# A scan kernel's broadcast load, taken from two stored copies, with its partitions ordered images by states

## The chip, the core and the metric

The kernel runs on one core of a Trainium2 chip. The metric is the device time of one execution in microseconds (us), as the median of several executions of the same build. The engines are named as in the profile: PE (matmul) and PEld (its weight load), DVE (vector), ACT (scalar activation), POOL (the general engine, here used for element-wise products) and SP, which issues nearly all DMAs. Sixteen DMA engines move the data of the core.

## What is computed

Four layers follow one another on 64 images of 11 x 11 = 121 tokens with 128 channels. Each layer is a mixer (a normalisation, then a state-space model) and a feed-forward part. Only the mixer is touched by the change. Its core, cut from the reference:

```python
xc = silu(conv1d(x @ in_proj_w.T) + conv_b)       # 121 rows d, 256 places l
delta = softplus(einsum('bkrl,kdr->bkdl', dts, dt_proj_w) + dt_proj_b)
dA  = exp(delta[..., None] * A)                   # 16 states n
dBu = delta[..., None] * Bs * xs[..., None]
h   = associative_scan(h[l] = dA[l] * h[l-1] + dBu[l], axis=l)
y   = einsum('bkdln,bknl->bkdl', h, Cs) + Ds * xs
y   = y[:, 0] + flip(y[:, 1])                     # two directions k
out = layer_norm(y) * gelu(z) @ out_proj_w.T
```

For each image b, direction k and row d there are 16 states n, each with a recurrence over 256 places.

## The kernel before

**Tiling.** A mixer treats the 64 images in 8 chunks c of 8 images. A chunk and a direction make one m (16 in a mixer). The 128 partitions hold 16 states times 8 images. In one step, `scan` (L701) runs the recurrence for two rows d on DVE: 128 partitions x 512 elements. An m has 61 steps, so a chunk has 122 and a mixer 976.

**What a step needs.** `rows` (L680) brings delta to the 128 partitions: a matmul of `pick` (a 0/1 matrix made in `made`, L148) with the tile `R`, into one of five PSUM tiles `da`. `exps` (L694) turns it into dA on ACT with the scale `A`, which is loaded with a broadcast over images (L135). The other factor starts as u = delta * x, in the layout rows d on partitions (`steps`, L293, product on POOL at L333). It is stored to DRAM in `uD` by `store` (L360). `load_u` (L658) reads four rows d of it for 8 images, 4 KB for each image, and writes them to all 128 partitions of a tile `ub`: one DMA of 512 KB, of which 31 belong to an m. `times_b` (L671) multiplies the tile in place by the tile `Bt` on POOL, and two steps of `scan` consume it. There are six `ub` tiles (`UB`); a load is issued 10 steps ahead of its first scan (`lu`) and the product 5 steps ahead (`tb`).

**After the scan.** `by_c` (L716) contracts the states with matmuls whose weights are `Cz`. These are made by `own_c` (L648) on POOL from the tile `Cp` and the mask `own` (L171), which says which partition belongs to which image. `keep_y` (L737) gathers the results in `yst`, `store_y` (L755) writes them to DRAM, and `tail` (L453) reads them back as `y` for the norm, the gate and the output product. `load_bc` (L640) loads `Bt` and `Cp`, `load_r` (L628) the tiles `R`, of which there are two.

**Order.** The order is written by hand. `run` (L779) files every piece of work under a step number; the numbers come from the table `AT` (L87). In each step the code issues in this order: work filed as `pre`, the matmuls and the first exp of three steps ahead, the loads and products of `ub`, the scan, the planned work, the second exp. Each engine executes its own instructions in that order. The work of the next chunk (normalisation, convolution, softplus, stores of `dD` and `uD`) and the tail of the previous one are spread over the 122 steps of a chunk, so a steady chunk repeats the same pattern. SP issues all these DMAs from one queue, in order, and waits ahead of each for its tiles: a `ub` load waits until DVE has scanned the tile six loads before.

Of the kernel before, what the change touches and what calls it, by code (L numbers as in the profile page):

```python
# [8 lines left out]
F32 = mybir.dt.float32  # L9
BF16 = mybir.dt.bfloat16  # L10
AF = mybir.ActivationFunctionType
ALU = mybir.AluOpType
AX = mybir.AxisListType
# [3 lines left out]
D = 121  # L17
C = 128
L = 256
NS = 16  # L20
# [20 lines left out]
def bcast(ap, n):  # L41

    return ap.unsqueeze(2).to_broadcast([ap.shape[0], ap.shape[1], n])
# [27 lines left out]
def act_tables(nc, which):  # L71
# [8 lines left out]
CB = 8  # L80
# [4 lines left out]
RING = 5  # L85
UB = 6
AT = {  # L87
    "x": -12.5, "st": -3, "mv": 3, "sc2": 6, "sc3": 8, "nm": 10, "tn": 13.5, "td": 15.5, "tn2": 17.5,
    "td2": 19.5, "cv": 20, "cve": 49, "silu": 52, "p0": 53, "pa0": 3.75, "s0": 66, "b0": 66, "ba0": 7.875,
    "p1": 100, "pa1": 2.25, "s1": 109, "b1": 111, "ba1": 7.5, "u": 4, "d0": 1, "r": 3, "d1": 5, "l": 6.5,  # L90
    "d2": 7, "dst": 12.5, "bc": 54, "bca": 3, "sk": 99, "ska": 2.5, "y0": 15.5, "y1": 35, "y2": 57.5, "y3": 82,
    "k0": 27, "k1": 44.5, "k2": 66.5, "k3": 89, "ka": 2, "ks": 2.5, "km": 4.5, "k2s": 6.5, "k3s": 9, "kn": 11,
    "kg": 13, "xa": 28.5, "xb": 66, "g0": 38, "z0": 77, "g1": 81.5, "z1": 109, "ga": 5, "za": 3.5, "gt": 117.5,
    "gta": 2, "ge": 126.5, "cz": 8, "cza": 3.75, "lbc": -18, "lu": 10, "tb": 5, "ys": 8, "ysa": 1, "ysh": 8,
    "r0": -10, "r1": 2, "r2": 23, "r3": 37,
}


class Conv:
# [9 lines left out]
    def weights(self, setup, fixed, ps):  # L109
        cx, nc, a = self.cx, self.nc, self.cx.a  # L110
        p = f"L{self.l}_conv_"

        def load(pool, name, shape, src):
            t = pool.tile(shape, F32, name=name)
            nc.sync.dma_start(t, src)
            return t

        in_x = load(setup, "in_x", [128, 2, C], a[p + "in_x"].rearrange("(q p) c -> p q c", p=128))
        conv_wT = load(
            setup, "conv_wT", [128, 3, 2, L], a[p + "conv_wT"].rearrange("j (q p) o -> p j q o", p=128)  # L120
        )
        x_dt = load(setup, "x_dt", [8, 2, D], a[p + "x_dt"])
        dt_wT = load(setup, "dt_wT", [8, 2, D], a[p + "dt_wT"])
        self.Ds = fixed.tile([128, 2], F32, name="Ds")
        nc.vector.memset(self.Ds, 0.0)
        nc.sync.dma_start(self.Ds[:D], a[p + "Ds"])
        self.in_zT = load(fixed, "in_zT", [C, L], a[p + "in_zT"])
        self.conv_b = load(fixed, "conv_b", [1, L], a[p + "conv_b"])
        self.x_bc = load(fixed, "x_bc", [D, 4 * NS], a[p + "x_bc"])
        self.norm = load(fixed, "norm", [D, 2], a[p + "norm"])  # L130
        self.out_wT = load(fixed, "out_wT", [128, 2, C], a[p + "out_wT"].rearrange("(q p) c -> p q c", p=128))

        self.A = fixed.tile([128, 2, D], F32, name="A")
        for k in range(2):
            nc.sync.dma_start(self.A[:, k, :], a[p + "A_logs"][k].unsqueeze(1).to_broadcast([NS, CB, D]))  # L135
        return lambda: self.made(setup, fixed, ps, in_x, conv_wT, x_dt, dt_wT)

    def made(self, setup, fixed, ps, in_x, conv_wT, x_dt, dt_wT):
        cx, nc, a = self.cx, self.nc, self.cx.a
        p = f"L{self.l}_conv_"  # L140
        af = self.A.rearrange("p k d -> p (k d)")
        nc.scalar.activation(af, af, AF.Exp)
        nc.vector.tensor_scalar_mul(af, af, -1.0)


        pick = setup.tile([5 * 24, 5, CB], F32, name="pick")
        nc.vector.reduce_sum(pick, cx.ident[:120, :120].rearrange("p (a s b) -> p a b s", s=3, b=CB), axis=AX.X)
        self.pick = fixed.tile([5 * 24, 5, NS, CB], BF16, name="pick16")  # L148
        for i in range(5):
            nc.vector.tensor_copy(self.pick[:, i], pick[:, i, :].unsqueeze(1).to_broadcast([120, NS, CB]))  # L150

        self.w_conv = fixed.tile([C, 3, L], F32, name="w_conv")
        for j in range(3):
            pw = ps.tile([C, L], F32, name="pw", tag="mm")
            for q in range(2):
                nc.tensor.matmul(pw, in_x[:, q, :], conv_wT[:, j, q, :], start=(q == 0), stop=(q == 1))
            nc.scalar.copy(self.w_conv[:, j, :], pw)


        self.w_dt = fixed.tile([D + 1, 2, 128], F32, name="w_dt")  # L160
        nc.vector.memset(self.w_dt, 0.0)
        nc.sync.dma_start(self.w_dt[D : D + 1, :, :D], a[p + "dt_b"].unsqueeze(0))
        for k in range(2):
            pw = ps.tile([D, D], F32, name="pdt", tag="mm")
            nc.tensor.matmul(pw, x_dt[:, k, :], dt_wT[:, k, :], start=True, stop=True)
            nc.scalar.copy(self.w_dt[:D, k, :D], pw)
        self.ones = fixed.tile([1, 128], F32, name="ones")
        nc.vector.memset(self.ones, 1.0)

        self.own = fixed.tile([128, CB], F32, name="own")  # L170
        nc.vector.reduce_sum(self.own, cx.ident.rearrange("p (n b) -> p b n", b=CB), axis=AX.X)  # L171

    def buffers(self, fixed, work, ps_f, dram):
        cx, nc, NC = self.cx, self.nc, self.NC
        self.work = work

        self.H = [fixed.tile([128, 2 * L, 16], F32, name="H"), cx.HX.rearrange("p (a w) -> p a w", w=16)]
        self.spare = [x.rearrange("p a w -> p (a w)") for x in self.H]
        self.da = [ps_f.tile([128, 2, L], F32, name=f"da{i}") for i in range(RING)]
        self.yb = ps_f.tile([128, 8, 2, 2, 16], F32, name="yb")  # L180
        nc.vector.memset(self.yb, 0.0)
        self.Cz = [fixed.tile([128, 64, CB], F32, name=f"Cz{i}") for i in range(4)]
        self.t = fixed.tile([128, CB, L], F32, name="t")
        nc.gpsimd.memset(self.t, 1.0)  # L184
        self.xnT = [fixed.tile([C, CB, D + 2], F32, name=f"xnT{i}") for i in range(2)]
        for x in self.xnT:
            nc.gpsimd.memset(x[:, :, 0 : D + 2 : D + 1], 0.0)
        self.skip = [fixed.tile([D, CB, L], F32, name=f"skip{i}") for i in range(2)]
        self.yst = fixed.tile([128, 64, D], F32, name="yst")
        self.uD = dram.tile([NC, 2, CB, 128, L], F32, name="uD")  # L190
        self.dD = dram.tile([NC, 2, 128, 3, CB, L], BF16, name="dD")
        self.bcD = dram.tile([NC, 4 * NS, CB, L], F32, name="bcD")
        self.yD = dram.tile([NC, L, CB * D], F32, name="yD")
# [99 lines left out]
    def steps(self, c, k, at=None):  # L293


        nc, work, out = self.nc, self.work, []
# [7 lines left out]
        for b in range(0, CB, 2):  # L304
            s = {}
# [53 lines left out]

            def store(b=b, s=s):  # L360
                nc.sync.dma_start(self.dD[c, k, :, :, b : b + 2, :].rearrange("d s b l -> d s (b l)"), s["d"])
                nc.sync.dma_start(
                    self.uD[c, k, b : b + 2].rearrange("b d l -> d b l"), s["u"].rearrange("p (b l) -> p b l", l=L)
                )

            i = b // 2
            fs = (u, first, rest, second, less, third, store)
# [272 lines left out]
    def load_bc(self, m):  # L640
        c, k = m // 2, m % 2
        for name, at in (("Bt", 0), ("Cp", NS)):
            x = self.work.tile([128, L], F32, name=name, bufs=2)
            r0 = 2 * NS * k + at
            self.nc.sync.dma_start(x, self.bcD[c, r0 : r0 + NS].rearrange("r b l -> (r b) l"))
            self.bc[m, name] = x

    def own_c(self, m, u):  # L648
# [9 lines left out]
    def load_u(self, T):  # L658
        m, i = divmod(T, TILES)
        n = min(4, D - 4 * i)  # L660
        x = self.work.tile([128, 4, L], F32, name="ub", bufs=UB)
        self.ub[T] = x
        self.nc.sync.dma_start(
            x[:, :n, :].rearrange("p d l -> p (d l)"),
            self.uD[m // 2, m % 2, :, 4 * i : 4 * i + n, :]
            .rearrange("b d l -> b (d l)")
            .unsqueeze(0)
            .to_broadcast([NS, CB, n * L]),
        )

    def times_b(self, T):  # L671
# [8 lines left out]
    def rows(self, g):  # L680

        m, p = divmod(g, PAIRS)
        for j in range(self.channels(p)):
            d = 2 * p + j
            n = 24 if d == D - 1 else 120
            self.nc.tensor.matmul(  # L686
                self.da[g % RING][:, j, 1:],
                self.pick[:n, d % 5].rearrange("p n b -> p (n b)"),
                self.R[m, d // 35][:n, d % 35 // 5, 1:],
                start=True,  # L690
                stop=True,
            )
# [802 lines left out]
```

## Time and profile before

| | |
|---|---|
| median of 3 runs | 7740.06 us (7738.5 to 7741.94) |
| profiled execution, own time | 7752.68 us |
| its span, first to last instruction | 7750.9 us |
| mean granted TensorE clock | 0.85 |
| PE, DVE, ACT, POOL busy, share of the span | 78%, 73%, 70%, 68% |
| DMA queue of SP, share of 16 engines | 76.3%, 1521.09 MB in 903223 packets |
| HBM read, written | 1265.98 MB, 256.97 MB |

The shares are averages over four mixers and four feed-forward parts. The mixers take about three quarters of the span. In a steady chunk (steps 122 to 975 of a mixer without the last chunk) the engines are far busier than the averages, so stretches of such a chunk have to be read by themselves. The chunk that is used below as the example runs from 2460.69 to 2643.87 us, in the second mixer.

### The profile page before, as it was taken

What the parts mean: (1) busy time and instruction counts of PE and PEld (TensorE: products, weight loads), DVE (VectorE), ACT (ScalarE), POOL (GpSimd) and SP (SyncE); (2) the same over time, 40 slices, a digit from 0 to 9 for tenths busy, and PEclk for the clock granted to TensorE, in tenths of its full rate; (3) what the DMA queues carried; (4) which work ended last, traced back from release to release, by engine and by line L of the source; (5) the groups of instructions that cost most, each with busy time, mean ns of one, the idle gap of its engine ahead of it and who ended that gap; (6) DMA issues with size and microseconds to landing.
All of it is one profiled execution on the core that took longest, in us unless ns stands there. A gap on an engine that the chain in (4) does not pass through costs nothing. (4 is left out here: it accounts for less than half of the span.)

```text
span 7750.9 us, 208787 instructions
## 1 busy us (share of the span) xinstructions
PE 6041.0 (78%) x84334; PEld 3448.5 (44%) x84334; DVE 5659.8 (73%) x7849; ACT 5449.4 (70%) x12343; POOL 5293.3 (68%) x2659
## 2 busy tenths in 40 slices
PE   6788778776788877766788888767678887758999
PEld 3444444465344444444344444434344444434445
DVE  5888888844788888962788888871788888872201
ACT  7888888733888888853788888862788888852200
POOL 6798999812888888931888888940888898960000
PEclk8888898777898989875889989875788888879999
DMA  7899999856899999942899999951899999971111
GB/s 181 227 247 243 245 246 243 215 167 170 221 241 249 246 240 244 247 110 75 220 241 244 246 248 243 243 140 37 217 236 243 243 245 241 245 184 46 35 39 36
DMA packets 905471, 1536.54 MB, mean 198 GB/s; under 512 B 136840, under 2 KB 617442, under 8 KB 904503
## 3 DMA queue, kind: packets, MB, share of 16 engines
q1 hardware_dynamic: 903223, 1521.09, 76.3%
q8 instruction: 662, 10.85, 0.6%
q14 instruction: 306, 2.51, 0.1%
q10 hardware_dynamic: 1280, 2.10, 0.1%
HBM read 1265.98 MB, written 256.97 MB: 196 GB/s over the span
## 5 line engine op out<-in xcount | busy, mean ns | idle before, releaser
L675 POOL TENSOR_TENSOR ub<-ub,Bt 128x1024 f32<-128x1024 f32 (+1 forms) x1984 | 4557.2, 2323 | 589.7 <-DMA ub<-uD 447.1
L699 ACT ACTIVATE da<-da,A 128x255 f32<-128x255 f32 x7744 | 3291.7, 451 | 696.1 <-PE da L686 612.0
L707 DVE TENSOR_TENSOR_SCAN H<-da,ub 128x512 f32<-128x512 f32 x2048 | 2391.8, 1208 | 354.4 <-POOL ub L675 183.9
L707 DVE TENSOR_TENSOR_SCAN HX<-da,ub 128x512 f32<-128x512 f32 (+1 forms) x1856 | 2130.4, 1190 | 318.5 <-POOL ub L675 160.1
L686 PE MATMUL da<-R,pick 120*128 120x255 bf16 x7744 | 1658.9, 305 | 546.0 <-DVE H L707 277.3
L686 PEld LDWEIGHTS <-pick 120*128 120x128 bf16 x7744 | 662.9, 103 | 1494.6 <-issue 1054.9
L728 PE MATMUL yb<-H,Cz 128*16 128x64 f32 x32768 | 782.2, 236 | 187.7 <-ACT yst L745 107.7
L728 PE MATMUL yb<-HX,Cz 128*16 128x64 f32 x32768 | 813.4, 237 | 122.6 <-DVE HX L707 62.7
L728 PEld LDWEIGHTS yb<-HX,Cz 128*16 128x16 f32 x32768 | 531.3, 105 | 641.9 <-issue 338.1
L728 PEld LDWEIGHTS yb<-H,Cz 128*16 128x16 f32 x32768 | 540.9, 103 | 584.0 <-issue 313.3
L263 PE MATMUL pc<-w_conv,xnT 128*121 128x256 f32 x1344 | 458.7, 433 | 27.4 <-ACT d L358 18.6
L184 POOL MEMSET t<- 128x2048 f32 x4 | 7.2, 1805 | 599.6 <-PE px L1221 211.8
L313 PE MATMUL pd<-t,w_dt 122*128 122x512 f32 x480 | 317.6, 749 | 101.7 <-ACT t L274 55.1
L745 ACT COPY yst<-yb 128x512 f32<-128x512 f32 (+2 forms) x640 | 334.9, 551 | 83.9 <-DMA yD<-yst 70.2
L743 DVE TENSOR_TENSOR yst<-yst,yb 128x512 f32<-128x512 f32 (+2 forms) x640 | 337.1, 543 | 73.7 <-PE yb L728 73.2
L340 PE MATMUL pr<-sp,ident 128*128 128x512 f32 x480 | 302.7, 717 | 80.0 <-ACT sp L301 75.0
L333 POOL TENSOR_TENSOR u<-sp,t 128x512 f32<-128x512 f32 x240 | 307.6, 1282 | 33.9 <-DMA uD<-u 32.8
L1294 DVE COPY U<-pu 128x488 f32<-128x488 f32 x128 | 85.4, 667 | 282.5 <-PE pu L1327 282.5
L1296 ACT COPY U<-pu 128x488 f32<-128x488 f32 x128 | 72.9, 570 | 308.7 <-PE pu L1327 308.7
L652 POOL TENSOR_TENSOR Cz<-Cp,own 128x512 f32<-128x512 f32 x256 | 275.5, 1076 | 0.0
L329 ACT CAST d<-sp 128x512 bf16<-128x512 f32 x240 | 148.6, 619 | 172.1 <-DMA dD<-d 171.9
L263 PEld LDWEIGHTS pc<-w_conv,xnT 128*121 128x121 f32 x1344 | 211.7, 194 | 94.9 <-ACT d L358 25.0
(237 smaller groups left out, 7243.8 us busy)
## 6 DMA issues: line engine op xcount, KB each, us to landing
ub<-uD SPq DMA_DIRECT2D x1920, 512.0 KB
dD<-d SPq DMA_DIRECT2D x256, 384.0 KB
R<-dD SPq DMA_DIRECT2D x192, 420.0 KB
uD<-u SPq DMA_DIRECT2D x256, 256.0 KB
yD<-yst SPq DMA_DIRECT2D x512, 60.5 KB
y<-yD SPq DMA_DIRECT2D x112, 242.0 KB
bcD<-bc SPq DMA_DIRECT2D x128, 128.0 KB
w1g<-in_L_ffn_weight_dram SPq DMA_DIRECT2D x16, 1024.0 KB
```

Of the source, the lines that this page charges most:

```text
L263: nc.tensor.matmul(pc, lhs, rhs, start=(j == 0), stop=(j == taps - 1))
L313: nc.tensor.matmul(s["p"], self.w_dt[:, k, :], tb[: D + 1], start=True, stop=True)
L333: nc.gpsimd.tensor_mul(s["u"], s["sp"], tb)
L340: nc.tensor.matmul(s["pr"], self.cx.ident, s["sp"], start=True, stop=False, skip_group_check=True)
L652: self.nc.gpsimd.tensor_mul(self.Cz[u], C.unsqueeze(2).to_broadcast([128, 64, CB]), self.own.unsqueeze(1).to_broadcast([128, 64, CB]),)
L675: self.nc.gpsimd.tensor_mul(x, x, self.bc[m, "Bt"].unsqueeze(1).to_broadcast([128, n, L]))
L686: self.nc.tensor.matmul(self.da[g % RING][:, j, 1:], self.pick[:n, d % 5].rearrange("p n b -> p (n b)"), self.R[m, d // 35][:n, d % 35 // ...
L699: self.nc.scalar.activation(x, x, AF.Exp, scale=self.A[:, m % 2, d : d + 1])
L707: self.nc.vector.tensor_tensor_scan(self.H[dq % 2][:, :n, p - DQ[dq][0]], self.da[g % RING].rearrange("p j l -> p (j l)")[:, :n], x.rearra ...
L728: self.nc.tensor.matmul(self.yb[32 * q : 32 * q + 16, slot % 8, :, :, :w], self.Cz[slot // 8][:, place % 64 : place % 64 + 2, :].rearrange ...
L743: nc.vector.tensor_add(dst, dst, src)
L745: nc.scalar.copy(dst, src)
```

## The change

`uD` gets one more dimension: each image's u is stored twice in DRAM, by two DMAs in the place of one. `load_u` then reads 16 rows (8 images x 2 copies), each to eight neighbouring partitions; before it read 8 rows and wrote the set of eight 16 times over. For this the partitions are ordered image by image with the 16 states inside, where they were state by state with the 8 images inside. `A`, `pick`, `own`, `Bt` and `Cp` follow the new order. Besides, 18 numbers of the table `AT` differ.

```diff
-    "x": -12.5, "st": -3, ... "tn": 13.5, "td": 15.5, ...
-    ... "silu": 52, ... "p1": 100, ... "u": 4, ... "d1": 5, ...
-    ... "y0": 15.5, ... "y2": 57.5, "y3": 82,
-    "k0": 27, ... "k2": 66.5, "k3": 89, ... "k2s": 6.5, ...
-    "xa": 28.5, ... "g0": 38, ... "gt": 117.5, ... "ge": 126.5,
-    "r0": -10, "r1": 2, "r2": 23, "r3": 37,
+    "x": -12.5, "st": -3, ... "tn": 12.5, "td": 14.5, ...
+    ... "silu": 51, ... "p1": 99.5, ... "u": 3, ... "d1": 4, ...
+    ... "y0": 17, ... "y2": 56.5, "y3": 82.5,
+    "k0": 26.5, ... "k2": 65.5, "k3": 89.5, ... "k2s": 6, ...
+    "xa": 30.5, ... "g0": 36, ... "gt": 114.5, ... "ge": 124.5,
+    "r0": -10, "r1": -6, "r2": 23, "r3": 37,
...
-            nc.sync.dma_start(self.A[:, k, :], a[p + "A_logs"][k].unsqueeze(1).to_broadcast([NS, CB, D]))
+            nc.sync.dma_start(self.A[:, k, :], a[p + "A_logs"][k].unsqueeze(0).to_broadcast([CB, NS, D]))
...
-        self.pick = fixed.tile([5 * 24, 5, NS, CB], BF16, name="pick16")
+        self.pick = fixed.tile([5 * 24, 5, CB, NS], BF16, name="pick16")
...
-        nc.vector.reduce_sum(self.own, cx.ident.rearrange("p (n b) -> p b n", b=CB), axis=AX.X)
+        nc.vector.reduce_sum(self.own, cx.ident.rearrange("p (b n) -> p b n", n=NS), axis=AX.X)
...
-        self.uD = dram.tile([NC, 2, CB, 128, L], F32, name="uD")
+        self.uD = dram.tile([NC, 2, CB, 2, 128, L], F32, name="uD")
...
-                nc.sync.dma_start(
-                    self.uD[c, k, b : b + 2].rearrange("b d l -> d b l"), s["u"].rearrange("p (b l) -> p b l", l=L)
-                )
+                for i in range(2):
+                    nc.sync.dma_start(
+                        self.uD[c, k, b : b + 2, i].rearrange("b d l -> d b l"),
+                        s["u"].rearrange("p (b l) -> p b l", l=L),
+                    )
...
-            self.nc.sync.dma_start(x, self.bcD[c, r0 : r0 + NS].rearrange("r b l -> (r b) l"))
+            self.nc.sync.dma_start(x, self.bcD[c, r0 : r0 + NS].rearrange("r b l -> b r l"))
...
+        rows = self.uD[m // 2, m % 2, :, :, 4 * i : 4 * i + n, :].rearrange("b i d l -> (b i) (d l)")
         self.nc.sync.dma_start(
-            x[:, :n, :].rearrange("p d l -> p (d l)"),
-            self.uD[m // 2, m % 2, :, 4 * i : 4 * i + n, :]
-            .rearrange("b d l -> b (d l)")
-            .unsqueeze(0)
-            .to_broadcast([NS, CB, n * L]),
+            x[:, :n, :].rearrange("p d l -> p (d l)"), rows.unsqueeze(1).to_broadcast([2 * CB, NS // 2, n * L])
         )
...
-                self.pick[:n, d % 5].rearrange("p n b -> p (n b)"),
+                self.pick[:n, d % 5].rearrange("p b n -> p (b n)"),
```

## The prediction

> **What bounds the kernel now.** I read the page first, then the stretches of one steady chunk, then its waits, then single stretches of DMA traffic.
>
> ```profile
> DVE  5888888844788888962788888871788888872201
> POOL 6798999812888888931888888940888898960000
> DMA  7899999856899999942899999951899999971111
> GB/s 181 227 247 243 245 246 243 215 167 170 221 241 249 246 240 244 247 110 75 220 241 244 246 248 243 243 140 37 217 236 243 243 245 241 245 184 46 35 39 36
> L675 POOL TENSOR_TENSOR ub<-ub,Bt 128x1024 f32<-128x1024 f32 (+1 forms) x1984 | 4557.2, 2323 | 589.7 <-DMA ub<-uD 447.1
> ub<-uD SPq DMA_DIRECT2D x1920, 512.0 KB
> ```
>
> In the mixers all 16 DMA engines are full, at about 245 GB/s, and two thirds of the 1536 MB are `ub` loads. POOL's product of `ub` waits 447 us for them in all. The example chunk by stretches (us, then PE, PEld, DVE, ACT, POOL busy, clock, DMA share, GB/s), cut at steps 24, 32, 48, 64, 72 and 104:
>
> ```profile
> 2460.69:2495.11 34.42, 27.00 (x482) 14.86 (x471) 31.23 (x45) 32.86 (x75) 33.32 (x19) 0.85 0.93 250
> 2495.11:2508.00 12.89, 10.42 (x126) 6.03 (x129) 9.76 (x13) 5.98 (x15) 9.77 (x5) 0.74 0.96 247
> 2508.00:2531.50 23.50, 22.99 (x343) 14.81 (x336) 20.51 (x24) 18.40 (x44) 21.59 (x11) 0.92 1.04 281
> 2531.50:2554.75 23.25, 18.40 (x320) 8.58 (x318) 18.48 (x25) 22.56 (x50) 17.88 (x10) 0.93 0.80 193
> 2554.75:2569.60 14.85, 9.94 (x183) 4.74 (x181) 11.05 (x14) 14.69 (x30) 14.22 (x7) 0.89 1.04 250
> 2569.60:2615.50 45.90, 35.60 (x674) 21.18 (x673) 45.43 (x60) 39.20 (x99) 45.16 (x25) 0.93 0.96 255
> 2615.50:2643.87 28.37, 22.66 (x408) 13.68 (x412) 27.07 (x34) 24.95 (x52) 23.34 (x12) 0.94 0.94 232
> ```
>
> Another engine is nearly full in each stretch but one: POOL, then (third line, the convolution) PE, then ACT twice (SiLU, softplus), then DVE. Only in the second line does nobody compute at the limit. There the waits are:
>
> ```profile
> DVE HX L707 <- POOL ub L675: 5.2, 5, 1.7
> POOL ub L675 <- DMA ub<-uD: 5.0, 6, 2.3
> ACT yst L745 <- DMA yD<-yst: 2.5, 1, 2.5
> ```
>
> (2485 to 2520 us.) DVE waits for POOL, and POOL for the loads. So the DMA engines are a bound, but one that sits close above three others.
>
> **Part 1, the load's source.** Is it the source that makes a `ub` load slow? Three stretches of DMA traffic with one kind of packet each: `ub` loads alone (67 to 77 us), the feed-forward's `m` loads, 128 rows of 1920 B, a row every 64 KiB (7001.6 to 7002.6 us), and `HX` loads, 121 rows of 4 KB, a row every 32 KiB (6951 to 6955 us):
>
> ```profile
> DMA packets 688, 2.49 MB, mean 249 GB/s; under 512 B 80, under 2 KB 80, under 8 KB 688
> q1 hardware_dynamic: 688, 2.49, 103.2%
> ...
> DMA packets 217, 0.36 MB, mean 361 GB/s; under 512 B 20, under 2 KB 217, under 8 KB 217
> q1 hardware_dynamic: 217, 0.36, 101.7%
> ...
> DMA packets 295, 1.10 MB, mean 274 GB/s; under 512 B 27, under 2 KB 27, under 8 KB 295
> q1 hardware_dynamic: 295, 1.10, 69.7%
> ```
>
> A 4 KB packet of `ub` takes 4096 x 16 / 249 = 263 ns. At the `m` loads' rate it would take 4096 x 16 / 361 = 182 ns. The `HX` loads show 4 KB packets at 4096 x 16 x 0.697 / 274 = 167 ns. Only `ub` has many DMA engines reading the same rows at once (8 rows for 16 engines); its writes go to 128 partitions as those of `m` do. I take 182 ns for the new load. Bounds: 160 ns, the quickest 4 KB packets of the trace, and 320 ns (next paragraph).
>
> A rule that speaks against the change: the Trainium skill, "DMA: Bandwidth & Descriptors", section "Latency and other measured facts", reports that copies slow down when rows lie a large power of two apart, from 207 GB/s at 512 KiB to 164 at 2 MiB and 103 at 4 MiB, half of the full 214. The 16 rows now lie 128 KiB apart, and the engines start on them together. The `m` rows, 64 KiB apart, show none of it (361 GB/s), and 128 KiB is below the page's list, so I follow the row. At half rate a packet would take 2 x 160 = 320 ns.
>
> What that is worth in DMA time: a chunk has 62 `ub` loads, 60.5 of full size, 8 packets for each DMA engine, so 484 packets. The trace's packet records give 255 ns for the mean over all, 123 us; the chunk's 183.2 us at a share of 0.95 are 174 us of DMA, so 51 us are other traffic. At 182 ns `ub` takes 88 us.
>
> **Part 2, the second store.** Eight more `uD<-u` DMAs in a chunk, 256 packets of 1 KB each at 52 ns (mean in the example chunk): 8 x 256 x 52 / 16 = 6.7 us. DMA sum: 51 + 88 + 7 = 146 us, 0.82 of 178. On SP they cost 8 x 0.62 us of issue (median of `uD<-u`); SP is idle over 90 us of the chunk, waiting for DVE to free `ub` (50.0 + 42.5 us), which hides it. In the prologue nothing does: four stores there delay the first loads, about 1 us in each mixer. POOL's `u` (L333) gets its buffer back some 1 us later; a buffer has 15 steps, so nothing.
>
> **Part 3, Bt, Cp and A.** Their source's slowest dimension becomes 8. The skill's same page, "Rules for kernel authors", says that an outermost dimension of c < 16 keeps a DMA on at most c engines. `HX` agrees: 121 rows, share 0.697 = 11/16. A `Bt` load then has 16 packets on each of 8 engines, 16 x 52 = 0.83 us for 0.42. By the page's rule that is 4 x 0.42 = 1.7 us in a chunk if it were on the path; it is issued 18 steps (27 us) ahead, so I take 0. `A` lies between layers. `pick`, `own` and the `Cz` products keep shape and count: 0.
>
> **Part 4, what the freed DMA time gives.** Per stretch, time less the busiest engine other than DMA: 1.1, 2.5, 0.5, 0.7, 0.2, 0.5, 1.3, in sum 6.8 us. I count the second and third in full (loads and `yst` stores end the waits), 1.1 of the first since POOL starts the second stretch with more lead, and half of the last (POOL waits for loads there, DVE hardly): 4.7 us. What is late next is PE in steps 32 to 48 and ACT at its two tables. Lower bound 2.5 (only the second stretch). Upper bound: every wait of DVE for POOL in this chunk (5.2 + 1.0 on `ub`, 3.6 on `Cz`), 9.8 us. 24 steady chunks: 24 x 4.7 = 113. The last chunk has no convolution: its steps 24 to 40 take 26.4 us with DVE, the busiest, at 20.7, so about 5 us of gain; the first starts with nine loads back to back at 2.1 us, now 1.5, also about 5 us: 4 x 10 = 40.
>
> **Part 5, the moved steps.** No step is added, so only waits can change. `r1` goes from 2 to -6: SP issues the 420 KB load of `R` ahead of four more `ub` loads, and its buffer is freed by the last `rows` of the previous m, so SP stands some 2 to 3 steps with the `ub` loads queued behind; they have 10 steps, and land in 3 to 4 us if DMA isn't backlogged: hidden. It leaves the fullest stretch (steps 0 to 8). `xa` +2 and `y0` +1.5 delay two loads past the yD stores and past `ub` loads; `xo` still has 10.5 steps, `y` 11.5. `silu`, `tn`, `td` one step earlier on ACT and PE; `gt`, `ge` 2 to 3 steps earlier move four copies and the gelu on ACT; `g0` stays within PE's full stretch, 2 steps sooner; `u` one step earlier on POOL, where it can wait for the softplus; `d1` one step nearer to its matmul; the `k` and `y2`, `y3` numbers move half a step or one. No row prices these. ACT, full in two stretches, may gain or lose one exp's wait in each: +/-1.5 us in a chunk, +/-48 us in all. Value 0, since both signs have a reason.
>
> **Sum.** 7752.7 - 113 - 40 + 4 = 7604 in the profiled execution. The median of the runs stands 0.16% below the profiled one (7740.06 / 7752.68), so 7590 us, 1.9% faster.
>
> **The rivals.**
> (a) The gain stays local: only the second stretch, 2.5 us x 32 less 4: 76 us, 7664. With the moved steps at their bad end (+48) it is 7712. For it: PE at 22.99 of 23.50 and ACT at 14.69 of 14.85.
> (b) POOL keeps its lead: once loads are early, no DVE wait for POOL is left: 9.8 x 32 = 314 us, 7430. For it: POOL idles 12.8 us of the chunk for loads; against: `Cz` and `u` still stand in its queue.
> (c) Slower: rows 128 KiB apart meet in the same part of memory. Break-even is where 484 packets take what they take now less the 6.7 us of stores: (123 - 7) / 484 = 240 ns. At 320 ns DMA needs 51 + 155 + 7 = 213 us, and the chunk is DMA-bound: 30 us x 32 = 950 us, 8690. At 255 ns DMA is full as today and pays 7 us of stores: at most 7 x 32 = 214 us, 7950.
> (d) It doesn't do what it says: the 4 KB packet itself is slow, whoever reads. `HX` loads of the third mixer (5160 to 5168 us) run at 175 GB/s on the same 11 engines, 263 ns. Then the second store alone is left, up to 7950 as above.
>
> **How the numbers follow.** Forecast 0.56; (a) 0.18, of which 0.05 ends within 0.2%; (b) 0.15; (c) 0.06; (d) 0.05. 0.2%, 15 us, is about what this kernel's measurement tells from none. Faster 0.56 + 0.13 + 0.15 = 0.84, same 0.05, slower 0.11. The range goes from 7430 (b) to 7735, which leaves out (c), (d) and a little of (a) and (b).
>
> **What would show it.** Right: `ub` alone near 350 GB/s at the start of a mixer; DMA share of a steady chunk near 0.82; POOL's wait for `ub` far under 447 us; the second stretch near 10.5 us, the third unchanged; HBM written up by 67 MB. Wrong: packets of 4 KB still near 255 ns, or POOL's waits for loads gone with a chunk still of 183 us (then PE or ACT holds it).

## The result and the profile after

The changed kernel is slower: 7786.68 us median (7776.55 to 7802.42, six runs) against 7742.36 us (7738.5 to 7758.48, six runs), ratio 1.0056, 95% interval 1.0043 to 1.0069. The forecast was 7590 us, 1.9% faster. The profiled execution took 7783.99 us, 31.3 us more than that of before, so the two traces can be compared directly.

The lines of the page that answer to those shown of before, and the two lines on queue and memory:

```profile
DVE  5888888843788888861789888871788888872201
POOL 6799888812888899930889888840788889960000
DMA  7899999856899999942899999951899999971111
GB/s 189 232 257 258 257 255 255 222 156 175 234 254 259 256 255 256 256 112 69 226 253 259 257 261 258 250 144 37 221 249 253 255 258 254 257 186 46 35 39 36
q1 hardware_dynamic: 971767, 1588.21, 75.7%
HBM read 1265.98 MB, written 324.08 MB: 204 GB/s over the span
L674 POOL TENSOR_TENSOR ub<-ub,Bt 128x1024 f32<-128x1024 f32 (+1 forms) x1984 | 4555.6, 2322 | 604.9 <-DMA ub<-uD 486.9
uD<-u SPq DMA_DIRECT2D x512, 256.0 KB
```

The DMA row is the same in all 40 slices. The mixers move about 10 GB/s more, which is the second store: 67 MB more written, as predicted. POOL's wait for the loads has not fallen but risen, 447 to 487 us.

The decisive view is the DMA traffic at the start of the first mixer, where `ub` loads run with next to nothing beside them (72 to 82 us; before, 67 to 77 us). The queue's line gives packets, MB and share:

```profile
DMA packets 683, 2.49 MB, mean 249 GB/s; under 512 B 76, under 2 KB 76, under 8 KB 683
q1 hardware_dynamic: 683, 2.49, 103.0%
```

It is the same 249 GB/s as before, where 350 were expected: 4096 x 16 x 1.03 / 249 = 271 ns for a packet. Over the whole run the packet records give a mean of 245 ns for a 4 KB packet, before 255: the sign of being wrong that the prediction names first.

The example chunk, cut at the same steps (0, 24, 32, 48, ...; us, then PE, PEld, DVE, ACT, POOL busy, clock, DMA share, GB/s):

```profile
2477.24:2510.61 33.37, 26.09 (x452) 14.32 (x441) 31.17 (x44) 31.11 (x70) 32.30 (x18) 0.80 0.97 264
2510.61:2525.46 14.85, 12.08 (x171) 7.51 (x169) 11.29 (x18) 8.82 (x21) 10.69 (x6) 0.89 0.98 278
2525.46:2549.44 23.98, 22.51 (x358) 14.25 (x358) 20.13 (x23) 20.13 (x49) 20.47 (x10) 1.00 1.03 257
```

In the second stretch nobody computes at the limit, and DMA is at 0.98, as it was. Averaged over the 24 steady chunks, a chunk takes 183.35 us at a DMA share of 0.947; before, 183.94 us at 0.955. So the steady chunks gained next to nothing, 0.6 us each or 14 us in all, and the first and last chunks of the mixers lost as much again: from first to last scan the four mixers differ by +5.4, +1.3, -3.7 and -2.9 us. The 31 us lie elsewhere: from the first `uD` store to the first scan of each mixer 4.4, 5.4, 5.9 and 6.0 us (21.7 in sum), and about 10 us in the reads of `HX` after the mixers. That code is the same in both kernels, but its packets drift: over 8 us of these reads after each mixer they take 203, 188, 257 and 212 ns in the trace of before, 199, 228, 248 and 249 in that of after. No row is shared there, so why they drift stays open.

Part of the starts can be seen in SP's timeline, first of before, then of after (start, duration, engine, line, operation):

```profile
60.38 0.39 SPq L636 DMA_DIRECT2D R<-dD  x1
60.86 3.93 SPq L663 DMA_DIRECT2D ub<-uD  x6
...
62.51 1.00 SPq L638 DMA_DIRECT2D R<-dD  x2
63.61 4.22 SPq L666 DMA_DIRECT2D ub<-uD  x6
```

With `r1` at -6 the second load of `R`, 420 KB, is filed ahead of the scans' first step, so in the first m of a mixer it goes ahead of the first `ub` load. From the first `ub` issue to the first product it was 6.3 us, and is 7.8 to 9.6.

### The profile page after: what moved, and what is told of

It is laid out like the page before. It is cut to its first block, busy times and chain, and to the rows that moved or that the text cites. A ratio compares the mean times of both kernels' runs of the same rounds, so it can differ in the third digit from the quotient of the medians.

```text
span 7782.2 us, 208842 instructions
## 1 busy us (share of the span) xinstructions
PE 6036.7 (78%) x84282; PEld 3443.4 (44%) x84334; DVE 5656.5 (73%) x7849; ACT 5458.0 (70%) x12343; POOL 5290.1 (68%) x2659
## 3 DMA queue, kind: packets, MB, share of 16 engines
q1 hardware_dynamic: 971767, 1588.21, 75.7%
## 4 chain that ended last, share of the span: by engine, by line
PE 27%; DMA 14%; ACT 14%; DVE 10%; issue 8%; POOL 7%; SPq 1%; DVEq 0%; POOLq 0%; ACTq 0%
DMA ub<-uD 8%; ACT da L698 7%; POOL ub L674 5%; DVE H L706 4%; PE yb L727 3%; PE pc L263 3%; DVE HX L706 3%; PE pu L1326 3%; PE acc L1329 3%; PE da L685 3%; PE out L1369 3%; DMA dD<-d 2%; PE pst L1213 2%; PE po L527 1%; DMA yD<-yst 1%
## 5 line engine op out<-in xcount | busy, mean ns | idle before, releaser
L263 PE MATMUL pc<-w_conv,xnT 128*121 128x256 f32 x1344 | 466.1, 439 | 24.3 <-ACT d L358 21.7
```

The lines of the kernel that those rows point to most:

```text
L263: nc.tensor.matmul(pc, lhs, rhs, start=(j == 0), stop=(j == taps - 1))
```

## The experiments

Each ratio is to the kernel before on the same chip, with its 95% interval. "Alone" is the mean of the packet records in the first microseconds of a mixer, from the lowest to the highest of the four mixers; "mean" is over all 4 KB packets of the run. "Chunk" and "share" are means over the 24 steady chunks (before: 183.94 us, 0.955; after: 183.35 us, 0.947). They are from one trace each, and the traces come from several chips, on which the median of the kernel before lies between 7741.5 and 7772 us (0.4%); a difference between chunks of under 0.7 us says little. Each expectation gives letters to its own theories.

### Is it the packet or its source?

The first question: can a 4 KB packet of `ub` be quick at all? One run gives each partition a row of its own, without any gap:

```diff
-        rows = self.uD[m // 2, m % 2, :, :, 4 * i : 4 * i + n, :].rearrange("b i d l -> (b i) (d l)")
...
+        flat = self.uD[m // 2, m % 2].rearrange("b i d l -> (b i d l)")
+        rows = flat[131072 * (i % 4) : 131072 * (i % 4) + 131072].rearrange("(p x) -> p x", p=128)
+        self.nc.sync.dma_start(x[:, :n, :].rearrange("p d l -> p (d l)"), rows[:, : n * L])
```

> The changed kernel with each ub load taken from 512 KB that lie in one piece in DRAM (128 partitions x 4 KB, nothing read twice); so u reaches the wrong rows and images, and only the time is of use. Theory W (the limit is on the write side, or in the 4 KB packet itself): ub loads alone at the start of a mixer stay at 236 to 256 GB/s, 4 KB packets near 245 ns in the mean, time within 0.5% of the changed kernel (7787 us). Theory S (the source pattern is the limit: rows a power of two apart, or read by several engines or several times): 340 GB/s or more alone, packets near 180 ns, and 100 to 200 us off the time.

Measured: 7666.18 us against 7771.99, ratio 0.9859 (0.9841 to 0.9876). Packets 180 to 183 ns alone, mean 204; chunk 180.06 us at share 0.831. Its page:

```profile
q1 hardware_dynamic: 971767, 1588.21, 66.4%
L673 POOL TENSOR_TENSOR ub<-ub,Bt 128x1024 f32<-128x1024 f32 (+1 forms) x1984 | 4553.2, 2324 | 446.9 <-DMA ub<-uD 359.5
```

The same packets and bytes as in the changed kernel take 66.4% of the engines' time in place of 75.7%. So 182 ns was right for a 4 KB packet on these partitions, and the source of the changed kernel is what makes it slow. POOL's wait falls by a quarter only.

### Pitch, distance, size

Three runs ask what in the source it is. A pitch of 132 KiB instead of 128:

```diff
-        self.uD = dram.tile([NC, 2, CB, 2, 128, L], F32, name="uD")
+        self.uD = dram.tile([NC, 2, CB, 2, 132, L], F32, name="uD")
```

> The changed kernel with the rows of uD 132 KiB apart in the place of 128 KiB. If the power of two is the limit: ub loads alone near 340 GB/s, packets near 180 ns, 100 to 200 us off. If it is the write side, the packet or the repeated reading: packets stay at 245 ns and the time within 0.5% of 7787 us.

Ratio 1.0029 (1.002 to 1.0038); 261 to 280 ns alone, mean 248; share 0.961. The pitch isn't it.

The 16 rows side by side, 64 KB in one piece, each still to eight partitions:

```diff
+        flat = self.uD[m // 2, m % 2].rearrange("b i d l -> (b i d l)")
+        rows = flat[16384 * i : 16384 * i + 16384].rearrange("(r x) -> r x", r=16)[:, : n * L]
```

> The changed kernel with the 16 rows of a ub load next to each other in DRAM (64 KB in one piece), each still written to eight partitions; u reaches the wrong rows, and only the time is of use. If reading a row again and again is the limit (theory R): ub alone stays at 236 to 265 GB/s, 4 KB packets near 245 ns in the mean, time within 0.5% of the changed kernel. If the distance of 128 KiB between the rows is the limit (theory D): packets near 180 ns alone, 204 in the mean, and 1.4 to 2% off as in the load from one piece.

Ratio 1.0023 (1.0009 to 1.0036); 254 to 279 ns alone, mean 246; share 0.960. And 128 different rows, of which 16 lie 128 KiB apart, with eight at every 16 KiB between:

```diff
+        rows = self.uD[m // 2, m % 2].rearrange("b i (j t e) l -> (b i) j t (e l)", t=4, e=4)[:, :, i % 4, : n * L]
+        self.nc.sync.dma_start(x[:, :n, :].rearrange("p d l -> p (d l)"), rows)
```

> The changed kernel with 128 different 4 KB rows in a ub load, none read twice, spread over 16 images' copies 128 KiB apart and, in each, 16 KiB apart; u reaches the wrong rows and partitions, and only the time is of use. Theory R (repeated reading): packets near 180 ns alone and 204 in the mean as in the load from one piece, 1.2 to 1.6% faster than before. Theory D (distance): packets stay near 245 ns, no gain.

Ratio 0.991 (0.9892 to 0.9928), 7694.75 us; 187 to 194 ns alone, mean 208; share 0.844. Rows far apart but not shared are quick, rows side by side but shared are slow. So distance and power-of-two pitch have little in it (e6 is 0.5% behind e1), and sharing has nearly all.

Two DMAs of two rows d each, packets of 2 KB:

```diff
+        for h in range(0, n, 2):
+            k = min(2, n - h)
+            d = 4 * i + h
+            rows = self.uD[m // 2, m % 2, :, :, d : d + k, :].rearrange("b i d l -> (b i) (d l)")
...
+                rows.unsqueeze(1).to_broadcast([2 * CB, NS // 2, k * L]),
```

> The changed kernel with each ub load split into two DMAs of two rows d, so 2 KB packets (256 packets for 128). If the 4 KB packet is the limit: the 2 KB packets take 85 to 95 ns and ub alone runs near 340 GB/s; against this stand 60 more issues of 0.5 us on SP in a chunk and the eight semaphores that SP's DMAs share, so the time is between -150 and +50 us. If the write ports or HBM are the limit whatever the packet: 125 to 130 ns per 2 KB packet, 250 GB/s, and the time 0 to +100 us.

Ratio 1.0026 (1.0018 to 1.0033), 7795.21 us; 2 KB packets 123 to 130 ns alone, mean 114; share 0.888. Alone, two of them take as long as one packet of 4 KB, so its size isn't what makes it slow; in the mean two take 228 ns in place of 245. The same edit on the kernel before:

> The kernel before with each ub load split into two DMAs of two rows d (2 KB packets), one store of u. In the changed kernel this split took DMA's share from 0.95 to 0.89 of a steady chunk and the time 0.3% down. If that carries over: 0.2 to 0.5% faster than before. If the 60 more issues and waits of SP in a chunk outweigh it: within 0.2%, or slower.

Ratio 0.9998 (0.999 to 1.0006), 7737.26 us; 107 to 134 ns alone, mean 116; share 0.874. Here the share of DMA in the steady chunk fell by 0.08 and the chunk by 0.4 us only: a lower share alone gave nothing. That the doubled number of DMAs in SP's one queue ate the gain is a guess.

### How many share a row, and which

The load of before with its eight rows side by side:

```diff
+        flat = self.uD[m // 2, m % 2].rearrange("b d l -> (b d l)")
+        rows = flat[8192 * i : 8192 * i + 8192].rearrange("(r x) -> r x", r=CB)[:, : n * L]
```

> The kernel before with the 8 rows of a ub load next to each other in DRAM (32 KB in one piece), still written 16 times over; u reaches the wrong rows, and only the time is of use. Theory R: packets stay at 255 ns in the mean (269 to 285 alone), time within 0.3% of before. Theory D: packets near 180 ns alone and 1.4% faster.

Ratio 0.9948 (0.993 to 0.9966), with packets as slow as before (275 to 279 ns alone, mean 254; share 0.960; chunk 182.55 us). The gain of 0.5% has no cause in the packets and stays unexplained. So part of what other loads from one piece gain may not come from their packets either: e6_far, whose rows lie apart, gains 0.9% where e1_contig gains 1.4%.

Then the number of partitions to a row, four and two in place of eight, rows side by side:

```diff
+        rows = flat[32768 * (i % 16) : 32768 * (i % 16) + 32768].rearrange("(r x) -> r x", r=32)[:, : n * L]
...
+            x[:, :n, :].rearrange("p d l -> p (d l)"), rows.unsqueeze(1).to_broadcast([32, 4, n * L])
```

> The changed kernel with 32 different 4 KB rows in a ub load, each written to 4 partitions (in one piece of 128 KB; u reaches the wrong rows, only the time is of use). Theory R1 (every further read of a row that is being read costs the same): the packet alone lies on a straight line in the number of repeats between 182 ns (1) and 266 ns (8), so 218 ns. Theory R2 (the limit is how many different rows are in flight; 16 and 8 rows give the same 266 ns): 266 ns still.

> As before with 64 different rows, each to 2 partitions (one piece of 256 KB). Theory R1: 194 ns alone. Theory R2: 230 to 266 ns. If two neighbouring partitions are read by the same DMA engine one after the other and that costs nothing: 182 ns, and 1.2 to 1.4% faster than before.

Four: 0.9881 (0.9862 to 0.99), 7649.07 us; 169 to 182 ns alone, mean 195; chunk 179.67 us, share 0.810. Two: 0.9901 (0.9881 to 0.9922); 173 to 189 ns alone, mean 198; share 0.814. Theories R1 and R2 both missed: the packet is neither slow whenever a row is read more than once, nor does its time go with the number of readings. The third case of e11_rep2, that reading by one engine in turn costs nothing, came for the packets; the time fell by 1.0% and not 1.2 to 1.4%. Between four and eight partitions there is a step from 169 to 182 ns (e10_rep4) to 254 to 279 ns (e5_near), and below it nothing. The stretches of DMA traffic at the start of the first mixer, e5_near (eight partitions; 76 to 82 us) and then e10_rep4 (four; 73.6 to 77 us):

```profile
DMA packets 403, 1.46 MB, mean 244 GB/s; under 512 B 46, under 2 KB 46, under 8 KB 403
q1 hardware_dynamic: 403, 1.46, 99.6%
...
DMA packets 377, 1.38 MB, mean 405 GB/s; under 512 B 41, under 2 KB 41, under 8 KB 377
q1 hardware_dynamic: 377, 1.38, 101.5%
```

Here the Trainium skill has the rule that was missing in the prediction: "DMA: Bandwidth & Descriptors", section "The descriptor swizzle", says that a DMA engine serves partitions in groups of four, neighbouring groups going to neighbouring engines. By that, a row for four partitions is read four times by one engine, and a row for eight by two engines that stand side by side and read it at the same time. The step lies where the rule puts it; the packet records do not say which engine moved a packet, so no trace here shows the assignment itself.

### Two engines at one row: the same reads with and without

One run repeats e3_two (two DMAs, 2 KB packets, 64 KB of source read eight times in all for a tile) with the source arranged as 32 pieces, each for four partitions (64 KB in one piece; the second DMA's begin one piece later):

```diff
+        for h in range(0, n, 2):
+            k = min(2, n - h)
+            f0 = 16384 * i + 256 * h
+            rows = flat[f0 : f0 + 16384].rearrange("(r x) -> r x", r=32)[:, : k * L]
...
+                x[:, h : h + k, :].rearrange("p d l -> p (d l)"), rows.unsqueeze(1).to_broadcast([32, 4, k * L])
```

> Two DMAs of 128 partitions for each ub load, as in the split into two rows each, but each reads 32 different pieces of 2 KB, each written to four neighbouring partitions, and both read the same 64 KB; so the bytes and the repeats are those of the changed load (64 KB, eight times), and within a DMA no two engines read the same piece if an engine has four neighbouring partitions at a time. u reaches the wrong rows, only the time is of use. Theory E (engines reading one row at the same time): 2 KB packets at 88 to 100 ns alone, where the split with shared rows took 125. Theory N (few different rows, or eight repeats): 125 ns.

Ratio 0.998 (0.997 to 0.9991), 7726.55 us against 7741.85; 91 to 96 ns alone, mean 100; chunk 181.97 us, share 0.816. The traffic of e3_two (74 to 80 us), then of e15_pieces (74 to 77 us), both full with 2 KB packets:

```profile
DMA packets 888, 1.62 MB, mean 270 GB/s; under 512 B 98, under 2 KB 98, under 8 KB 888
q1 hardware_dynamic: 888, 1.62, 105.8%
...
DMA packets 629, 1.15 MB, mean 383 GB/s; under 512 B 68, under 2 KB 68, under 8 KB 629
q1 hardware_dynamic: 629, 1.15, 104.3%
```

The size of the packets, their number and how often the bytes of a tile are read are the same, and the rate goes from 270 to 383 GB/s. If an engine has four neighbouring partitions at a time, no two engines take one row at once here, and that is the likely cause of the quicker packets. The two runs differ in one thing more: a DMA of e3_two reads 16 different pieces, 128 KiB apart, eight times each, one of e15_pieces 32 pieces side by side four times each. Distance is excluded for 4 KB packets (e5_near). That fewer than 32 different pieces in a DMA, or eight readings of each, are slow whoever reads is not excluded: no run gives 16 rows to one engine each. The gain in time is less than in e10_rep4, at nearly the same DMA share (0.816 and 0.810): a chunk takes 2.3 us more, with 60 more DMAs in it.

Two runs in which the tile was loaded in two halves of 64 partitions, to let each row go to four partitions with two stored copies only:

```diff
+        for h in range(2):
+            self.nc.sync.dma_start(
+                x[64 * h : 64 * h + 64, :n, :].rearrange("p d l -> p (d l)"),
+                rows.unsqueeze(1).to_broadcast([2 * CB, 4, n * L]),
+            )
```

> The changed kernel with each ub load split into two DMAs of 64 partitions; each reads the 16 rows (8 images x 2 copies) and writes every row to four neighbouring partitions. The partitions are ordered half of the states, image, eight states, and A, pick, own, Bt and Cp follow; everything is computed. Theory E (what costs is that two DMA engines read one row at the same time, and an engine has four neighbouring partitions at a time): 4 KB packets near 182 ns alone and 200 in the mean, DMA share of a steady chunk 0.81 to 0.84, and 0.3 to 1.3% faster than before (the load from 32 rows gave 1.2% with 62 loads in a chunk; here SP has 62 more issues of 0.5 us). Theory N (the limit is the number of different rows in a load, 16 being too few, or that a row is read eight times): 245 ns in the mean as in the changed kernel, 0.3 to 0.8% slower than before.

Ratio 1.0165 (1.015 to 1.0179), 7895.02 us; 267 to 284 ns alone, mean 250. Read by itself it speaks against theory E. But the halves are slow without any sharing too. The next run loads them from rows of their own:

```diff
+        for h in range(2):
+            ps = slice(64 * h, 64 * h + 64)
+            self.nc.sync.dma_start(x[ps, :n, :].rearrange("p d l -> p (d l)"), rows[ps, : n * L])
```

> The load from one piece (128 different rows of 4 KB, each read once; u reaches the wrong rows, only the time is of use) with each ub load split into two DMAs of 64 partitions. If a DMA on 64 partitions is slow by itself [...], the packets alone are at 260 to 300 ns though no row is read twice, and the run with two halves and 16 rows says nothing on the rows. If not, 180 ns, as undivided, and that run stands for theory N (too few different rows).

Ratio 1.0375 (1.0348 to 1.0401), 8031.04 us; 261 to 283 ns alone, mean 259; share 0.985. Whole, the same source gave 180 ns (e1_contig). So e13_halves can't tell anything about sharing. The skill's "SBUF — State Buffer", section "Door 1: The DMA port swizzle", would explain it by the write ports that 64 neighbouring partitions reach, half of all; the packets take about one and a half times as long here, and no run shows the ports themselves.

### The store and the steps

The kernel before with a second store of u to a tensor that nobody reads:

```diff
+        self.uE = dram.tile([NC, 2, CB, 128, L], F32, name="uE")
...
+                for t in (self.uD, self.uE):
```

> The kernel before with a second store of u into a tensor that nobody reads. If the second store is what costs the changed kernel its 0.56%: first scan of a mixer 3 to 6 us later after its first store of u, and +20 to +45 us in all. If not (the new load, the order of partitions or the steps): within 10 us of before.

Ratio 1.0101 (1.0085 to 1.0117), 7842.71 us against 7768.22: 75 us for a store that the prediction had at 4, and more than the 20 to 45 us expected here. Chunk 185.86 us, 1.9 more than before; the mixers 14 to 22 us longer each; their starts (first `uD` store to first scan) 1.5 to 2.4 us.

```profile
HBM read 1265.98 MB, written 324.08 MB: 203 GB/s over the span
L677 POOL TENSOR_TENSOR ub<-ub,Bt 128x1024 f32<-128x1024 f32 (+1 forms) x1984 | 4555.3, 2321 | 657.0 <-DMA ub<-uD 512.8
```

The steps by themselves, first the kernel before with the new table `AT`, then the changed kernel with the old one:

> The kernel before with the 18 new numbers of the table of steps alone. If the steps cost the time: +20 to +45 us on 7742. If the stores, the prologue and the load's source cost it: within 15 us of 7742.

> The changed kernel with the 18 old numbers of the table of steps. If the steps do nothing, as in the kernel before: 0.4 to 0.7% slower than before, as the changed kernel. If they were chosen for the new traffic (longer stores, R loaded earlier) and pay there: 0.8 to 1.2% slower than before, near the second store alone (1.01%).

On the kernel before: 0.9995 (0.9985 to 1.0005), chunk 183.65 us. In the changed kernel, with the old steps: 1.0087 (1.007 to 1.0104), 7809.89 us, chunk 184.81 us. So the new steps do nothing to the kernel before, and may give the changed one about 0.3% (1.0087 against 1.0056, each against runs of the kernel before on its own chip; the intervals just part, and the changed kernel with another pitch, e2_pad, had 1.0029, so runs on other chips differ by as much). They make each start longer: by 2.2 to 3.0 us on the kernel before, and by 2.2 to 2.8 us in the changed one. Most of it is the load of `R`: from the first `ub` issue to the first product it is 8.0 to 8.3 us with the new steps alone, 6.3 before.

### The version that follows from it

If a row has to go to four partitions, 8 images need four stored copies. This kernel stores u four times and reads 32 rows:

```diff
-        self.uD = dram.tile([NC, 2, CB, 2, 128, L], F32, name="uD")
+        self.uD = dram.tile([NC, 2, CB, 4, 128, L], F32, name="uD")
...
-            x[:, :n, :].rearrange("p d l -> p (d l)"), rows.unsqueeze(1).to_broadcast([2 * CB, NS // 2, n * L])
+            x[:, :n, :].rearrange("p d l -> p (d l)"), rows.unsqueeze(1).to_broadcast([4 * CB, NS // 4, n * L])
```

> The changed kernel with u stored four times, each ub load reading 32 rows (8 images x 4 copies) to four partitions each; everything is computed. The load from 32 rows with two stores was 1.2% faster than before. With packets at 182 ns alone and DMA at 0.85 of a steady chunk, two more stores cost 2 x 5 us in each mixer's start and 1 to 2 us in a chunk: 0.2 to 0.8% faster than before. If more stores cost as much as the second one did (1%): 0.5 to 0.9% slower.

Ratio 1.007 (1.0055 to 1.0085), 7795.4 us; packets 184 to 188 ns alone, mean 202; chunk 183.47 us, share 0.877; starts 7 to 9 us later. It is the second of the expected cases: more stores cost as much as the second one did. Lines of e10_rep4, then of e16_four:

```profile
q1 hardware_dynamic: 971767, 1588.21, 64.7%
HBM read 1265.98 MB, written 324.08 MB: 208 GB/s over the span
L675 POOL TENSOR_TENSOR ub<-ub,Bt 128x1024 f32<-128x1024 f32 (+1 forms) x1984 | 4554.2, 2327 | 438.3 <-DMA ub<-uD 360.4
...
q1 hardware_dynamic: 1111031, 1722.46, 70.2%
HBM read 1265.98 MB, written 458.29 MB: 222 GB/s over the span
L674 POOL TENSOR_TENSOR ub<-ub,Bt 128x1024 f32<-128x1024 f32 (+1 forms) x1984 | 4551.1, 2321 | 552.8 <-DMA ub<-uD 449.7
```

The packets are quick here, in a kernel that computes everything. But with the two further stores (134 MB) POOL's wait is back at 450 us and the chunk at 183.47 us, from 179.67. Some 0.7 of these 3.8 us may come from the rows, which lie apart again (e6_far against e1_contig: 180.74 and 180.06 us). No complete kernel of these beats the one before by more than a measurement can tell.

## Why the prediction was wrong, step by step

**What bounds the kernel: held.** With quick unshared loads the time falls (e1_contig, e10_rep4: 1.2 to 1.4%), so the `ub` loads are a bound, and it is close above others: taking the share from 0.95 to 0.81 gave no more than 4.3 us of a chunk.

**Part 1 failed, and with it the sign.** The step that failed is "I take 182 ns for the new load": its packets took 271 ns alone in the first mixer and 245 in the mean, before 255. 182 ns itself was right for a row that isn't shared in this way (180 to 183 in e1_contig, 184 to 188 in e16_four), and the prediction's reason, many engines reading the same rows at once, is supported by e10_rep4 and e15_pieces. What is not written down there is the assumption that 16 rows for 16 engines make an engine the only reader of its row. By the skill's rule above eight neighbouring partitions are two engines' share, and a row for two engines cost as much as a row of before, which by the same rule has eight. A look at which partitions an engine serves would have shown it. The skill's rule on rows a large power of two apart was set aside there, rightly: at 128 KiB it shows nothing (e2_pad, e5_near).

**Part 2 was mis-sized by a factor of nearly 20.** The store was priced at 4 us, only its place in the prologue, because DMA was to have room at 0.82 and SP's idle 90 us were to cover its issues. With the queue full as it stayed, it costs 75 us of the median (e7_store2). In the profiled execution the four mixers are 73 us longer: 1.9 us in each of 24 steady chunks make 46, the first chunks add 18 (4.5 each) and the last ones 9; the starts, 1.5 to 2.4 us each where about 1 was predicted, come on top. The prediction had the size for this case, 6.7 us of DMA time in a chunk, in its rivals; 1.9 of them reach the end. That cover would have been thin even with quick loads: from e10_rep4 to e16_four the share goes from 0.81 to 0.88, and the chunk with 16 more stores takes up to 3.8 us more.

**Part 3 held for the engines, and missed the starts.** `Bt` and `Cp` do load on half of the engines now. At the start of the first mixer, before (60.7 to 61.4 us), then after (62.6 to 63.3 us):

```profile
q1 hardware_dynamic: 189, 0.18, 92.4%
...
q1 hardware_dynamic: 131, 0.13, 52.1%
```

(`HX`, which the prediction names beside the rule, is no case of it, since 121 is not under 16.) The prediction's 0 rests on the 18 steps by which the loads go ahead; at a mixer's start they don't have them. The new order wasn't tried alone. Between e7_store2 and e9_after_oldsteps lie the load's new source and this order; the starts grow by 1.1 us, and the ratio goes from 1.0101 to 1.0087, within the intervals.

**Part 4 was nearly right on what it priced, for loads that didn't come.** 4.7 us in a steady chunk were expected; e10_rep4, with the second store in it, gives 183.94 - 179.67 = 4.3. By stretch, as means over the steady chunks in the prediction's order, e10_rep4 gives 1.0, 1.5, 1.0, -0.1, 0.4, 0.5 and 0.0 us against 1.1, 2.5, 0.5, 0, 0, 0 and 0.65. The example chunk of e10_rep4 in its third and fourth stretch:

```profile
2485.93:2506.92 20.99, 20.60 (x324) 13.27 (x316) 20.09 (x22) 16.89 (x43) 19.81 (x10) 1.00 0.96 323
2506.92:2530.86 23.94, 19.14 (x353) 8.86 (x351) 19.10 (x25) 23.66 (x53) 19.99 (x11) 0.93 0.62 203
```

With DMA at 0.62 ACT holds the fourth, 23.66 of 23.94 us, and PE the third: what was named as late next was so. The first chunks gave nothing in e1_contig where 5 us were expected, the last ones the 5.

**Part 5: the value 0 held on the kernel before**, and the load of `R` ahead of the first `ub` loads, which was looked at in a steady m only, cost most of the 2 to 3 us by which each start grew.

**The rivals.** (a) and (b) start from quick loads; e10_rep4, which has them, gains 4.3 us in a chunk, between (a)'s 2.5 and (b)'s 9.8. (d) ended nearest, with its "second store alone is left", at 0.05; its reason, a 4 KB packet that is slow whoever reads, is refuted for `ub` (e1_contig); for `HX`, from which it was taken, the slow packets stay unexplained. (c) is refuted too (e2_pad, e5_near), though its case of 255 ns described what came: packets as slow as before, and the stores on top. The fault of the forecast lies in the chance of this case: "the load doesn't get quicker" had 0.11 in all, on a count of readers that was never made.

**The sum as measured.** The second store costs 1.0% (1.0101), with the new source and order it is 1.0087, with the new steps 1.0056. Of the three differences only the first is clear of noise. The traces go the same way: from before over e7_store2 and e9_after_oldsteps to after a steady chunk takes 183.94, 185.86, 184.81 and 183.35 us, and a start 25.1, 27.0, 28.0 and 30.6 us on average. So what the store cost in the steady chunks came back, and the loss left in the trace is the starts. Left open are the 0.5% of e8_before_near, and why POOL still waits some 11 us of a chunk for loads (example chunk of e10_rep4, 11.7 us) when DMA has room. The runs with more DMAs (e12_before_two, e15_pieces, e16_four) point to SP's single queue, in which a `ub` load stands behind stores; no run isolates it.

## What to carry to other kernels

Before storing copies so that a broadcast load reads more rows, write down which engine reads which row: here loads with a row for four neighbouring partitions, by the skill's rule one reader, ran at 400 GB/s, and with a row for eight, two readers, at 250, no better than eight readers. Price the copies' own traffic at what the queue's state makes of it: here each further store of 67 MB went with about 1% of the kernel, so that the three more which unshared rows need ate all that they brought. And a bound relieved gives only the distance to the next one: a fifth off the mean time of the largest stream's packets (245 to 195 ns) took DMA from 0.95 to 0.81 of a chunk, and 2% off the chunk.

## What was not expected of the hardware

- A load that writes each row of DRAM to eight neighbouring partitions takes 254 to 279 ns for a 4 KB packet (e5_near), as much as the load of before; one that writes it to four takes 169 to 182 ns (e10_rep4), no more than one that reads each row once (180 to 183 ns, e1_contig). Two engines at one row at the same time are the likely reason.
- Two DMAs to 64 partitions each, one issued after the other, take 261 to 283 ns for a 4 KB packet from rows read once (e14_contig_halves), one DMA to 128 partitions 180 to 183 ns (e1_contig).
- A stored copy that nobody reads cost 1.0% where the DMA engines stood at 0.955 of a steady chunk (e7_store2).
